# The attention output projection as seven products of quarters through one accumulator bank

## The chip, the core and the metric

The kernel runs on one core of a Trainium2 chip. The metric is the device time of one execution in microseconds; three executions of the kernel before the change took 3067.99, 3068.76 and 3071.80 us, median 3068.76 us. In addition one execution was recorded by the hardware profiler, instruction by instruction; every duration below comes from that record.

The engines are named as the profile names them: PE is the matrix engine (PEld its weight loads), DVE is VectorE, ACT is ScalarE, POOL is GpSimd, SP is SyncE, which here issues nearly all DMAs. Each engine works through its own instructions in program order; between engines, semaphores make an instruction wait for what it needs. PE writes its sums to eight PSUM banks of 128 x 512 fp32 values, and DVE and ACT read them from there.

## What is computed

Two layers. Layer 0 is a small graph attention; the change does not touch it. Layer 1 is a transformer block with a modulated layer norm, for four batches of 1024 rows of 512 values, 16 heads of 64:

```python
mod = jax.nn.silu(c) @ W_mod + b_mod
sh_msa, sc_msa, g_msa, sh_mlp, sc_mlp, g_mlp = jnp.split(mod, 6, axis=-1)
x = x + g_msa * _attention(_modulate(_layernorm(x), sh_msa, sc_msa), W_qkv, W_out, b_out)
x = x + g_mlp * _ff(_modulate(_layernorm(x), sh_mlp, sc_mlp), W1, b1, W2, b2)
```

with

```python
def _attention(x, W_qkv, W_out, b_out):
    q, k, v = jnp.split(x @ W_qkv, 3, axis=-1)          # each to 16 heads of 64
    attn = jax.nn.softmax(jnp.einsum('bqhd,bkhd->bhqk', q, k) * DH ** (-0.5), axis=-1)
    out = jnp.einsum('bhqk,bkhd->bqhd', attn, v).reshape(Bq, Tq, INNER)   # INNER = 1024
    return out @ W_out + b_out
```

The change concerns `out @ W_out`, the product of 1024 x 1024 by 1024 x 512 for each batch.

## The kernel before

**Stages.** Layer 0 and the modulation take the first 420 us or so, attention runs to about 2255 us, and the MLP to the end. All matmuls are fp32; the profile shows each as two records (and two weight loads).

**Attention is a row of 256 steps.** A step is one row tile of 128 queries (8 per batch) of one pair of heads (8 pairs `gp` per batch, 4 batches; `NS` = 256). Two pairs form a group `g` of 256 inner columns; there are 16 groups. Step `s` issues, in this order of the program: the transpose `turn` (L1118) of the first head of step s-1, evacuations left over in `later`, the two heads' `scores` (L1083, K = 64, two heads side by side in the array, into the four banks `psc`), their two row maxima `largest` on DVE (L1094), the exponentials `weights` on ACT (L1100), the reciprocal and the scaling `scaled` (first head L1107 on ACT, second head L1109 on POOL), the transpose of the second head of step s-1, and then the *fill* of the step.

**Transposed weights.** DVE transposes 32 x 32 blocks into a staging buffer `wd` (one per head and two row tiles, two buffers each, four in all); then SP issues four DMAs per head that bring the quarters to their partitions in `wT`. `attend` (L1045) multiplies `wT` of two row tiles by `v`, 16 matmuls of 256 columns into a bank `pav`, and ACT copies the result to `oT` (L1054).

**Fill.** What lies outside softmax is a list of entries (earliest step, latest step, units of PE time, place within the step, function): projections to q, k and v (each weight product by seven products of quarters, L498, in the two banks `q1` and `q2`, four entries in a fixed `chain`), `attend` (place 1), the output projection `project` (place 2), loads (place 0), sums and gates on POOL (place 4). `order_chain` places the chain by dynamic programming and `order_others` the rest, so that the squares of the units per step are smallest; `emit` writes a step's entries in the order of their places, where a chain entry has place 0.5, or 2.5 if the step before has one too.

**Output projection.** For each group, `project(b, g, n)` multiplies one row tile of the two pairs' `oT` by two 128-row pieces of `wout` (two matmuls of 512 columns, accumulated in a bank), and DVE adds the bank to the residual rows `xr[b, n]` (L1071). `wout` was multiplied by the gate g_msa on POOL beforehand (L959), and `xr` got the gated bias (L969). `pav` and `pout` share two banks under one tag, `mm`. After the last group of a batch, the rows' statistics are taken and the rows stored to `x2d`.

**MLP.** The next block of 512 rows is prepared in four pieces: `norm_T` transposes a piece in four 128-column matmuls on PE into one of two banks alternately (L408), and DVE applies scale and shift (L415). This is called in `between()`, after the first of the seven down products.

Of the kernel before, what the change touches and what calls it, by code (L numbers as in the profile page):

```python
# [41 lines left out]
def cond_block_kernel(  # L42
# [879 lines left out]
    ps = pctx.enter_context(tc.tile_pool(name="ps2", bufs=1, space=PSUM))  # L922
    with ExitStack() as actx:
        ap_ = actx.enter_context(tc.tile_pool(name="ap", bufs=1, reuse_waits="tile"))
        MM = dict(tag="mm", bufs=2)
        q1, q2 = (ps.tile([P, F], F32, name=n, tag=n) for n in ("q1", "q2"))
        two_banks = {"ma": q2, "mb": q1, "mc": q1, "md": q2}
        NP = 2 * NGRP
# [6 lines left out]
        wout, gate = {}, {}  # L935
        vt, oT, xr, wn, wd, wT = {}, {}, {}, {}, {}, {}

        def bank(name):
            return ps.tile([P, F], F32, name=name, **MM)

        turns = []

        def bank_q(name):
# [4 lines left out]

        def load_out(b, g):

            t = op_.tile([P, 2, F], F32, name="wout", tag="wout", bufs=1)
            nc.sync.dma_start(t, w_out[g * GW : (g + 1) * GW, :].rearrange("(c p) f -> p c f", p=P))
            wout[b, g] = t

# [3 lines left out]
            for p in range(2):  # L958
                nc.gpsimd.tensor_tensor(t[:, p, :], t[:, p, :], gate[b][0], ALU.mult)  # L959

        def load_rows(b, n):

            t = op_.tile([P, F], F32, name="xr", tag="xr", bufs=NT)
            nc.sync.dma_start(t, x1d[b * NT + n])
            xr[b, n] = t

        def gate_rows(b, n):

            nc.gpsimd.tensor_tensor(xr[b, n], xr[b, n], gate[b][1], ALU.add)  # L969


        def gates_of(b):
# [62 lines left out]
                rhs=lambda which, n, c: of_weights(("v", b, g), wv[b, g], which, c),  # L1035
            )

        def attend(b, gp, k):

            po = ps.tile([P, QB], F32, name="pav", **MM)  # L1040
            g, p = divmod(gp, 2)
            w = wT[b, gp, k]
            for m in range(KC):
                for j in range(2):
                    nc.tensor.matmul(  # L1045
                        po[j * D : (j + 1) * D, :],
                        lhsT=vt[b, g][:, m, p * P + j * D : p * P + (j + 1) * D],
                        rhs=w[:, j, :, m, :],
                        start=(m == 0),
                        stop=(m == KC - 1),  # L1050
                    )
            if k == 0:
                oT[b, gp] = op_.tile([P, S], F32, name="oT", tag="oT", bufs=3)
            nc.scalar.copy(  # L1054
                oT[b, gp][:, k * QB : (k + 1) * QB].rearrange("p (t u q) -> p u t q", t=QT, u=4),
                po.rearrange("p (u t q) -> p u t q", t=QT, u=4),
            )

        def project(b, g, n):

            po = ps.tile([P, F], F32, name="pout", **MM)
            for p in range(2):
                nc.tensor.matmul(  # L1063
                    po,
                    lhsT=oT[b, 2 * g + p][:, n * P : (n + 1) * P],
                    rhs=wout[b, g][:, p, :],
                    start=(p == 0),
                    stop=(p == 1),
                )
            t = xr[b, n]  # L1070
            nc.vector.tensor_tensor(t, po, t, ALU.add)  # L1071
            if g == NGRP - 1:
                i = b * NT + n
                statistics(t, mv2[:, i, :], op_)
                nc.sync.dma_start(x2d[i], t)


        def scores(b, gp, t):
# [32 lines left out]
        def turn(b, gp, t, j):  # L1111

            k, at = divmod(t, QT)
            if at == 0:
                wd[j] = ap_.tile([P, 4 * KC, QT, U], F32, name="wd", tag=f"wd{j}", bufs=2)
                if j == 0:
                    wT[b, gp, k] = ap_.tile([P, 2, 4, KC, QT * U], F32, name="wT", tag="wT", bufs=2)
            nc.vector.transpose(wd[j][:, :, at, :], wn.pop((b, gp, t, j)).rearrange("p (m k) -> p m k", k=U))  # L1118
# [9 lines left out]
            return lambda: qp.tile([P, S], F32, name="ex", tag=tag, bufs=2)  # L1128

        def home_o():  # L1130
            return op_.tile([P, S], F32, name="ex", tag="oT", bufs=3)

        def home_v():
            return vp.tile([P, NT, GW], F32, name="hs", tag="v", bufs=2)
# [10 lines left out]
        NS = B * NP * NT  # L1145
        LAG = 4

        chain = []
# [18 lines left out]
        for b in range(B):  # L1167
# [22 lines left out]
            for gp in range(NP):  # L1190
# [13 lines left out]

                for k in range(NB):
                    lo = at + QT * k + LAG
                    add(lo, lo + (lo < NS - 8), 2, 1, attend, b, gp, k)
                if p == 1:
                    for n in range(NT):
                        lo = at + max(QT * (n // 2) + LAG + 2 + (g == 0), 7)  # L1210
                        hi = at + 19
                        if at == NS - NT:

                            lo = hi = NS + (-2, -1, -1, 0, 1, 1, 3, 3)[n]
                        add(lo, hi, 1, 2, project, b, g, n)
                if gp == 0:
                    lo = max(at - 1, 0)
                    add(lo, lo, 0, 0, gates_of, b)
                    for n in range(NT):

                        lo = at + (1 + n if b == 0 else 14 + n // 2)
                        add(lo, lo, 0, 0, load_rows, b, n)
                        add(lo + 1, lo + 1, 0, 4, gate_rows, b, n)
                if p == 0:
                    add(at + 12, at + 12, 0, 0, load_out, b, g)
                    add(at + 13, at + 13, 0, 4, gate_out, b, g)
# [23 lines left out]
        add(NS - 7, NS - 7, 0, 0, put_w1_rows)  # L1250
        add(NS - 8, NS - 8, 0, 4, mlp_rows)
        for i in range(4):
            at = NS - (10, 9, 6, 4)[i]
# [17 lines left out]


        where = [f[0] for f in fill]
        inside = set(chain)

        def takes(k):

            return fill[k][2], int(k not in inside and fill[k][3] in (1, 2))

        def load_of(ks):  # L1280
            used = {}
# [3 lines left out]
            return used  # L1285

        def cost_of(u, n):
            return u * u + 4 * max(n - 2, 0) ** 2

        def order_chain():  # L1290

            used = load_of(k for k in range(len(fill)) if k not in inside)
            values = {where[k] for k, f in enumerate(fill) if f[3] == 1}
            first_steps = set(range(0, len(chain), 4))
            best = {(0, 0): (0, ())}
            for s in range(-8, NS):
                new = {}
                for (n, was), (cost, at) in best.items():
                    load, banks = used.get(s, (0, 0))
                    for m in range(2):  # L1300
                        extra = 0
                        if m > 0:
                            if n == len(chain) or not fill[chain[n]][0] <= s <= fill[chain[n]][1]:
                                break
                            load += fill[chain[n]][2]
                            if was and n not in first_steps and s not in values:
                                extra = 3
                        if n + m < len(chain) and fill[chain[n + m]][1] <= s:
                            continue
                        c = cost + cost_of(load, banks) + extra  # L1310
                        if (n + m, m) not in new or c < new[n + m, m][0]:
                            new[n + m, m] = c, (at, (s,) * m)
                best = new
            at = min((best[k] for k in best if k[0] == len(chain)), key=lambda v: v[0])[1]
            slots = []
            while at:
                at, part_ = at
                slots.append(part_)
            for k, s in zip(chain, [s for part_ in reversed(slots) for s in part_]):
                where[k] = s  # L1320
# [21 lines left out]
                    used[where[k]] = used.get(where[k], (0, 0))[0] + u, used.get(where[k], (0, 0))[1] + n  # L1342

        for _ in range(4):
            order_chain()
            order_others()
        for k, n, late in behind:
            where[k] = where[n] + late
# [12 lines left out]
        def emit(a, b):  # L1361


            for s in range(a, b):
                steps = {where[k] for k in chain}

                def place(k):
                    if k in inside:
                        return 2.5 if s - 1 in steps else 0.5
                    return fill[k][3]  # L1370

                for k in sorted(fill_of(s), key=lambda k: (place(k), k)):
                    fill[k][4]()
                if s in steps and s - 1 not in steps and sum(fill[k][2] for k in fill_of(s)) >= 3:
                    while later:
                        later.pop(0)()

        row_sum(0, 2)
        emit(-3, 0)
        before = None  # L1380
        for s in range(NS + 1):
# [4 lines left out]
            if s < NS:  # L1386
                b, r = divmod(s, NP * NT)
                gp, t = divmod(r, NT)
                sc = scores(b, gp, t)
                mx = [largest(sc[j]) for j in range(2)]  # L1390
                ws = [weights(sc[j], mx[j]) for j in range(2)]
                now = ((b, gp, t), ws)
                scaled(0, *ws[0])
# [38 lines left out]
    with ExitStack() as mctx:  # L1432
# [53 lines left out]
        for k in range(NB2):  # L1486
# [33 lines left out]
            def between():  # L1520
                if nxt < NB2:
                    for c in range(FC):
                        norm_T(1, nxt, c, new_bank, on_act=False)
                if k * VB % NT == 0:
                    spread(2, b, gate2)
                    spread(3, b, bias2)
# [79 lines left out]
```

## Time and profile before

| | |
|---|---|
| median of three executions | 3068.76 us |
| profiled execution, its time | 3070.33 us |
| profiled execution, span from first to last instruction | 3068.5 us |
| granted PE clock, mean | 0.999 of full |
| output projection on PE (L1063), records, mean of one | 512, 609 ns |
| adds of it on DVE (L1071) | 128, 678 ns |
| maxima on DVE (L1094) | 512, 1211 ns |
| transposes on DVE (L1118) | 512, 1237 ns |
| scaling on POOL (L1109) | 256, 2843 ns |
| sums of quarters on POOL (L469 to L472, 128x256) | 33 each for q and k, 728 to 730 ns |
| chain that ended last, PE's share | 82% |

The rows of a group say how long one instruction was in flight. Matmuls are pipelined, so the time that a matmul takes from PE is the distance between the starts of two that follow each other, not the 609 ns of the table. In a timeline row the columns are: start and length in us, engine, line, operation, what it writes and reads, shapes, how many were merged, and in brackets the idle time of the engine before it with what ended it.

### The profile page before, as it was taken

How to read it: one execution, taken by the hardware profiler on the slowest of the kernel's cores; microseconds unless marked ns; L12 is line 12 of the kernel's file. 1: busy time of each engine (PE TensorE's matmuls, PEld its weight loads, DVE VectorE, ACT ScalarE, POOL GpSimd, SP SyncE). 2: the span in 40 equal slices, each digit the busy share in tenths (PEclk: the TensorE clock that was granted, in tenths of full speed). 3: DMA queues.
4: the chain of work that ended last, by engine and by line, in shares of the span. 5: the costliest groups of instructions: out<-in, count | busy, mean ns of one | idle time of the engine just before them, and what ended most of it. 6: DMA issues, size and time to landing. Idle time of an engine off the chain costs nothing.

```text
span 3068.5 us, 40812 instructions
## 1 busy us (share of the span) xinstructions
PE 3032.4 (99%) x14977; PEld 1921.3 (63%) x14977; DVE 1972.2 (64%) x2759; ACT 1423.0 (46%) x2351; POOL 1212.8 (40%) x742
## 2 busy tenths in 40 slices
PE   9999999999999999999999999999999999999999
PEld 5666655455455455455455455455468888888888
DVE  3788867777878777878777878777864232223222
ACT  2444455555755555755555756556641221112211
POOL 1444456454555555555545555555531100111010
PEclk9999999999999999999999999999999999999999
DMA  6343448667777777777776777776872010101110
GB/s 194 123 131 107 137 100 202 154 159 174 190 182 189 176 168 168 194 181 181 181 174 161 197 184 175 181 177 149 194 198 80 14 46 30 49 14 42 35 41 14
DMA packets 282714, 418.00 MB, mean 136 GB/s; under 512 B 28912, under 2 KB 101036, under 8 KB 282516
## 3 DMA queue, kind: packets, MB, share of 16 engines
q1 hardware_dynamic: 282268, 415.06, 53.1%
q8 instruction: 120, 1.97, 0.3%
q14 instruction: 78, 0.64, 0.1%
q10 hardware_dynamic: 248, 0.34, 0.0%
HBM read 121.09 MB, written 25.76 MB: 48 GB/s over the span
## 4 chain that ended last, share of the span: by engine, by line
PE 82%; DVE 6%; ACT 3%; POOL 2%; issue 2%; DMA 2%; SPq 2%; POOLq 0%; ACTq 0%; DVEq 0%
PE q L498 18%; PE psc L1083 15%; PE pav L1045 14%; PE pout L1063 7%; PE mbd L498 5%; PE mbu L498 5%; PE mad L498 3%; PE mau L498 3%; PE mcd L498 2%; PE mdd L498 2%; ACT w L1100 2%; PE mcu L498 2%; PE mdu L498 2%; POOL t L727 1%; PE pa L704 1%
## 5 line engine op out<-in xcount | busy, mean ns | idle before, releaser
L1109 POOL TENSOR_SCALAR w<-w,sm 128x1024 f32<-128x1024 f32 x256 | 727.8, 2843 | 849.0 <-DVE sm L1105 849.0
L1100 ACT ACTIVATE w<-psc,mx 128x1024 f32<-128x1024 f32 x512 | 571.6, 1116 | 634.0 <-DVE mx L1094 632.7
L1118 DVE STREAM_TRANSPOSE wd<-w 128x1024 f32<-128x1024 f32 x512 | 633.4, 1237 | 131.4 <-ACT w L1107 113.5
L1094 DVE TENSOR_REDUCE mx<-psc 128x1 f32<-128x1024 f32 x512 | 599.4, 1211 | 122.0 <-PE psc L1083 119.9
L1083 PE MATMUL psc<-kT,qT 64*128 64x512 f32 x2048 | 530.8, 615 | 3.1 <-ACT kT L1009 1.4
L1045 PE MATMUL pav<-wT,v 128*64 128x256 f32 x4096 | 477.0, 382 | 2.6 <-DMA wT<-wd 2.3
L1045 PEld LDWEIGHTS pav<-wT,v 128*64 128x64 f32 x4096 | 294.5, 137 | 223.2 <-issue 68.3
L1083 PEld LDWEIGHTS psc<-kT,qT 64*128 64x128 f32 x2048 | 203.7, 186 | 254.8 <-issue 145.4
L1107 ACT ACTIVATE w<-w,sm 128x1024 f32<-128x1024 f32 x256 | 291.6, 1139 | 0.0
L477 POOL TENSOR_TENSOR tx<-hT 128x512 f32<-128x512 f32 x8 | 10.2, 1269 | 600.8 <-DVE hT L415 600.8
L1063 PE MATMUL pout<-wout,oT 128*128 128x512 f32 x512 | 245.5, 609 | 0.0
L498 PE MATMUL q<-hT,wqk 128*128 128x512 f32 (+1 forms) x396 | 182.6, 585 | 4.5 <-DVE q L512 4.5
L1063 PEld LDWEIGHTS pout<-wout,oT 128*128 128x128 f32 x512 | 90.2, 189 | 134.0 <-issue 119.0
L520 ACT COPY mbu<-mau 128x512 f32<-128x512 f32 x30 | 17.2, 572 | 276.4 <-PE mau L498 276.4
L704 PE MATMUL pa<-kp,sfT 128*128 128x320 f32 x512 | 143.5, 433 | 1.7 <-ACT sfT L679 1.7
L1071 DVE TENSOR_TENSOR xr<-pout,xr 128x512 f32<-128x512 f32 x128 | 85.5, 678 | 79.8 <-PE pout L1063 79.7
L498 PEld LDWEIGHTS q<-hT,wqk 128*128 128x128 f32 x396 | 73.5, 190 | 100.7 <-issue 86.5
L498 PE MATMUL q<-tx,ex 128*128 128x512 f32 (+1 forms) x264 | 125.0, 597 | 0.4 <-POOL tx L477 0.4
L704 PEld LDWEIGHTS pa<-kp,sfT 128*128 128x128 f32 x512 | 94.8, 190 | 38.5 <-ACT sfT L679 2.2
L664 PE MATMUL pf<-wx,xT 128*128 128x512 f32 x256 | 116.2, 597 | 0.9 <-DVE pf L653 0.9
L498 PE MATMUL mad<-w,hs 128*128 128x256 f32 x512 | 113.1, 379 | 0.0
L498 PEld LDWEIGHTS mad<-w,hs 128*128 128x128 f32 x512 | 97.3, 190 | 13.2
(285 smaller groups left out, 4234.5 us busy)
## 6 DMA issues: line engine op xcount, KB each, us to landing
wT<-wd SPq DMA_DIRECT2D x1024, 256.0 KB
wqk<-in_w_qkv SPq DMA_DIRECT2D x64, 256.0 KB
xT<-in_xt SPq DMA_DIRECT2D x32, 256.0 KB
xs<-in_x SPq DMA_DIRECT2D x32, 256.0 KB
x1d<-xs SPq DMA_DIRECT2D x32, 256.0 KB
xl<-x1d SPq DMA_DIRECT2D x32, 256.0 KB
wv<-in_w_qkv SPq DMA_DIRECT2D x32, 256.0 KB
xr<-x1d SPq DMA_DIRECT2D x32, 256.0 KB
```

The costliest lines, as they stand in the source:

```text
L498: nc.tensor.matmul(t[:, q * width : (q + 1) * width], lhsT=lhs(which, q, k), rhs=rhs(which, q, k), start=(fresh and q == 0 and k == 0), st ...
L664: nc.tensor.matmul(pfs[i], lhsT=xT[i][:, c, :], rhs=wx[:, c, :], start=False, stop=(c == FC - 1), skip_group_check=True,)
L704: nc.tensor.matmul(pas[i][:, n, :HF], lhsT=sfT2[i][:, c, :], rhs=kp[:, b, c, n * HF : (n + 1) * HF], start=False, stop=(c == FC - 1), skip ...
L1045: nc.tensor.matmul(po[j * D : (j + 1) * D, :], lhsT=vt[b, g][:, m, p * P + j * D : p * P + (j + 1) * D], rhs=w[:, j, :, m, :], start=(m == 0),
L1063: nc.tensor.matmul(po, lhsT=oT[b, 2 * g + p][:, n * P : (n + 1) * P], rhs=wout[b, g][:, p, :], start=(p == 0), stop=(p == 1),)
L1071: nc.vector.tensor_tensor(t, po, t, ALU.add)
L1083: nc.tensor.matmul(sc[j][:, n * F : (n + 1) * F], lhsT=qT[b, gp][q, t * P : (t + 1) * P], rhs=kT[b, gp][q, n * F : (n + 1) * F], start=Tru ...
L1094: nc.vector.tensor_reduce(mx, sc, axis=AX.X, op=ALU.max, negate=True)
L1100: nc.scalar.activation(w, sc, AF.Exp, bias=mx, accum_out=sm)
L1107: nc.scalar.mul(w, w, sm)
L1109: nc.gpsimd.tensor_scalar(w, w, sm, None, ALU.mult)
L1118: nc.vector.transpose(wd[j][:, :, at, :], wn.pop((b, gp, t, j)).rearrange("p (m k) -> p m k", k=U))
```

## The change

**Output projection.** For 15 of the 16 groups, `project` is replaced by `out_step`. The rows of a batch are taken in two halves `u` of 512 rows. Each half of the group's product (512 x 256 by 256 x 512) is cut into quarters and made by seven products instead of eight (Winograd's form of Strassen's scheme): `out_sums` makes three sums of quarters of `oT` (and changes one quarter in place), `out_weights` three of `wout`, both on POOL, four instructions each. Each product is two matmuls of 256 columns that fill one bank `pu`. The products are ordered so that the bank accumulates from one to the next; after each, DVE adds the whole bank to one quarter of `xr`. The last group keeps `project`.

**Banks.** The tag `mm` with its two banks goes; `pu` and `pav` get one bank each.

**Placing.** The 14 entries of a group (0.5 units each) form a second chain `outs` that `order_chain` places too, now with up to two in a step. If a step has two, `early` issues the first right behind the step's maxima. The weights in the search change as well. `attend` of the seventh pair of each batch is cut in two halves in two steps.

**Buffers.** The staging buffers `wd` of both heads share three instead of four; `wout` has two buffers and is loaded four steps earlier; `xr` holds two row tiles a tile; `oT` is six tiles of half the size.

**MLP.** In `between()`, `norm_T` applies scale and shift on ACT for all four pieces in the first block and for every second piece in the others.

```diff
-            t = op_.tile([P, 2, F], F32, name="wout", tag="wout", bufs=1)
+            t = op_.tile([P, 2, F], F32, name="wout", tag="wout", bufs=2)
...
-            t = op_.tile([P, F], F32, name="xr", tag="xr", bufs=NT)
-            nc.sync.dma_start(t, x1d[b * NT + n])
+            t = op_.tile([P, 2, F], F32, name="xr", tag="xr", bufs=NT // 2)
+            for r in range(2):
+                nc.sync.dma_start(t[:, r, :], x1d[b * NT + 2 * m + r])
...
-            po = ps.tile([P, QB], F32, name="pav", **MM)
+            if a == 0:
+                pav[0] = ps.tile([P, F], F32, name="pav", tag="pav")[:, :QB]
+            po = pav[0]
...
+        PU = ((1, 1, (0, 0)), (0, 1, (0, 0)), (5, 0, (0, 1)), (6, 0, (1, 1)), (3, 0, (1, 0)), (4, 1, (1, 1)), (2, 0, (0, 1)))
+        def out_weights(b, g):
+            w = wout[b, g]
+            wsum[b, g] = op_.tile([P, 3 * HB], F32, name="wsum", tag="wsum", bufs=1)
+            o = [wsum[b, g][:, k * HB : (k + 1) * HB] for k in range(3)]
+            sums_b(nc.gpsimd, o, w[:, 0, :HB], w[:, 0, HB:], w[:, 1, :HB], w[:, 1, HB:])
+        def out_sums(b, g, u):
+            osum[b, g] = op_.tile([P, 3 * HB], F32, name="osum", tag="osum", bufs=1)
+            o = [osum[b, g][:, k * HB : (k + 1) * HB] for k in range(3)]
+            l, r = (oT[b, 2 * g + p, u] for p in range(2))
+            sums_a(nc.gpsimd, o, l[:, :QB], r[:, :QB], l[:, QB:], r[:, QB:])
+        def out_step(b, g, u, k):
+            which, fresh, (i, j) = PU[k]
+            if fresh:
+                pu[0] = ps.tile([P, F], F32, name="pu", tag="pu")
...
+            for q in range(2):
+                nc.tensor.matmul(
+                    pu[0][:, q * HB : (q + 1) * HB],
+                    lhsT=a[:, q * P : (q + 1) * P],
+                    rhs=r,
+                    start=(bool(fresh) and q == 0),
+                    stop=True,
+                    skip_group_check=True,
+                )
+            o = xr[b, 2 * u + i][:, :, j * HB : (j + 1) * HB]
+            nc.vector.tensor_tensor(o, pu[0].rearrange("p (r f) -> p r f", r=2), o, ALU.add)
...
-                wd[j] = ap_.tile([P, 4 * KC, QT, U], F32, name="wd", tag=f"wd{j}", bufs=2)
+                wd[j] = ap_.tile([P, 4 * KC, QT, U], F32, name="wd", tag="wd", bufs=3)
...
+                    for u in range(2):
+                        for k in range(len(PU)):
+                            lo, hi = ((at + 8, at + 12), (at + 12, at + (15 if at == NS - 3 * NT else 17)))[u]
+                            if k == 0:
+                                behind.append((len(fill), len(fill) + 1, 0))
+                                add(-1, -1, 0, 4, out_sums, b, g, u)
+                            outs.append(len(fill))
+                            add(lo + k, hi + k, 0.5, 2, out_step, b, g, u, k)
...
         def cost_of(u, n):
-            return u * u + 4 * max(n - 2, 0) ** 2
+            return u * u + 4 * max(n - 1, 0) ** 2
...
-                    for m in range(2):
-                        extra = 0
+                    for m in range(2 if apart else 3):
+                        extra = 0.2 * (m == 2)
...
                 def place(k):
                     if k in inside:
-                        return 2.5 if s - 1 in steps else 0.5
+                        at = 2.5 if s - 1 in steps else 0.5
+                        return at if k in chain else min(at, 2) + 0.1 if s in steps else 2
...
+        def early(s):
+            two = [k for k in outs if where[k] == s]
+            if len(two) > 1:
+                fill[two[0]][4]()
+                done_early.add(two[0])
...
                 sc = scores(b, gp, t)
                 mx = [largest(sc[j]) for j in range(2)]
+                early(s)
                 ws = [weights(sc[j], mx[j]) for j in range(2)]
...
-                        norm_T(1, nxt, c, new_bank, on_act=False)
+                        norm_T(1, nxt, c, new_bank, on_act=(k == 0 or c % 2 == 1))
```

More of the change, by code (lines that the diff above doesn't have):

```diff
@@ L924, in cond_block_kernel @@
         ap_ = actx.enter_context(tc.tile_pool(name="ap", bufs=1, reuse_waits="tile"))
-        MM = dict(tag="mm", bufs=2)
         q1, q2 = (ps.tile([P, F], F32, name=n, tag=n) for n in ("q1", "q2"))
@@ L936, in cond_block_kernel @@
         vt, oT, xr, wn, wd, wT = {}, {}, {}, {}, {}, {}
-        def bank(name):
-            return ps.tile([P, F], F32, name=name, **MM)
         turns = []
@@ L959, in gate_out, with load_rows, gate_rows @@
                 nc.gpsimd.tensor_tensor(t[:, p, :], t[:, p, :], gate[b][0], ALU.mult)
-        def load_rows(b, n):
-            t = op_.tile([P, F], F32, name="xr", tag="xr", bufs=NT)
-            nc.sync.dma_start(t, x1d[b * NT + n])
-            xr[b, n] = t
-        def gate_rows(b, n):
-            nc.gpsimd.tensor_tensor(xr[b, n], xr[b, n], gate[b][1], ALU.add)
+        def load_rows(b, m):
+            t = op_.tile([P, 2, F], F32, name="xr", tag="xr", bufs=NT // 2)
+            for r in range(2):
+                nc.sync.dma_start(t[:, r, :], x1d[b * NT + 2 * m + r])
+            xr[b, m] = t
+        def gate_rows(b, m, r):
+            nc.gpsimd.tensor_tensor(xr[b, m][:, r, :], xr[b, m][:, r, :], gate[b][1], ALU.add)
         def gates_of(b):
@@ L1036, in v_steps, with attend @@
             )
-        def attend(b, gp, k):
-            po = ps.tile([P, QB], F32, name="pav", **MM)
+        pav = {}
+        def attend(b, gp, k, a=0, z=KC):
+            if a == 0:
+                pav[0] = ps.tile([P, F], F32, name="pav", tag="pav")[:, :QB]
+            po = pav[0]
             g, p = divmod(gp, 2)
             w = wT[b, gp, k]
-            for m in range(KC):
+            for m in range(a, z):
                 for j in range(2):
@@ L1051, in attend @@
                     )
-            if k == 0:
-                oT[b, gp] = op_.tile([P, S], F32, name="oT", tag="oT", bufs=3)
+            if z < KC:
+                return
+            u, i = divmod(k, 2)
+            if i == 0:
+                oT[b, gp, u] = op_.tile([P, F], F32, name="oT", tag="oT", bufs=6)
             nc.scalar.copy(
-                oT[b, gp][:, k * QB : (k + 1) * QB].rearrange("p (t u q) -> p u t q", t=QT, u=4),
+                oT[b, gp, u][:, i * QB : (i + 1) * QB].rearrange("p (t u q) -> p u t q", t=QT, u=4),
                 po.rearrange("p (u t q) -> p u t q", t=QT, u=4),
@@ L1059, in project @@
         def project(b, g, n):
-            po = ps.tile([P, F], F32, name="pout", **MM)
+            name = ("pu", "pav")[n % 2]
+            po = ps.tile([P, F], F32, name=name, tag=name)
             for p in range(2):
@@ L1064, in project @@
                     po,
-                    lhsT=oT[b, 2 * g + p][:, n * P : (n + 1) * P],
+                    lhsT=oT[b, 2 * g + p, n // 4][:, n % 4 * P : (n % 4 + 1) * P],
                     rhs=wout[b, g][:, p, :],
@@ L1069, in project, with rows_out @@
                 )
-            t = xr[b, n]
+            t = xr[b, n // 2][:, n % 2, :]
             nc.vector.tensor_tensor(t, po, t, ALU.add)
[L1072 to L1075, printed above, removed]
+            rows_out(b, n)
+        def rows_out(b, n):
+            t, i = xr[b, n // 2][:, n % 2, :], b * NT + n
+            statistics(t, mv2[:, i, :], op_)
+            nc.sync.dma_start(x2d[i], t)
@@ new lines, in cond_block_kernel @@
+        osum, wsum = {}, {}
+        PU = ((1, 1, (0, 0)), (0, 1, (0, 0)), (5, 0, (0, 1)), (6, 0, (1, 1)), (3, 0, (1, 0)), (4, 1, (1, 1)), (2, 0, (0, 1)))
[9 more added lines that the diff above has]
+            sums_a(nc.gpsimd, o, l[:, :QB], r[:, :QB], l[:, QB:], r[:, QB:])
@@ new lines, in cond_block_kernel @@
+        pu = {}
+        def out_step(b, g, u, k):
+            which, fresh, (i, j) = PU[k]
+            if fresh:
+                pu[0] = ps.tile([P, F], F32, name="pu", tag="pu")
+            if which in SUM_A:
+                a = osum[b, g][:, SUM_A[which] * HB : (SUM_A[which] + 1) * HB]
+            else:
+                h, f = {0: (0, 0), 1: (0, 1), 3: (1, 1), 6: (1, 0)}[which]
+                a = oT[b, 2 * g + f, u][:, h * QB : (h + 1) * QB]
+            if which in SUM_B:
+                r = wsum[b, g][:, SUM_B[which] * HB : (SUM_B[which] + 1) * HB]
+            else:
+                f, h = {0: (0, 0), 1: (1, 0), 2: (1, 1), 6: (0, 1)}[which]
+                r = wout[b, g][:, f, h * HB : (h + 1) * HB]
+            for q in range(2):
[9 more added lines that the diff above has]
+            nc.vector.tensor_tensor(o, pu[0].rearrange("p (r f) -> p r f", r=2), o, ALU.add)
@@ L1130, in home_o @@
         def home_o():
-            return op_.tile([P, S], F32, name="ex", tag="oT", bufs=3)
+            return op_.tile([P, 3 * HB], F32, name="ex", tag="wsum", bufs=1)
         def home_v():
@@ L1146, in cond_block_kernel @@
         LAG = 4
-        chain = []
+        chain, outs = [], []
         def add(lo, hi, units, place, f, *args):
@@ L1206, in cond_block_kernel @@
                     lo = at + QT * k + LAG
+                    if gp == NP - 2:
+                        for h in range(2):
+                            add(lo + h, lo + h, 1, 1, attend, b, gp, k, h * KC // 2, (h + 1) * KC // 2)
+                        continue
                     add(lo, lo + (lo < NS - 8), 2, 1, attend, b, gp, k)
-                if p == 1:
+                if p == 1 and at == NS - NT:
                     for n in range(NT):
[L1210 to L1215, printed above, removed]
+                        lo = NS + (-2, -1, -1, 0, 1, 1, 3, 3)[n]
+                        add(lo, lo, 1, 2, project, b, g, n)
+                elif p == 1:
+                    if outs:
+                        behind.append((len(fill), outs[-1], 0))
+                        add(-1, -1, 0, 4, out_weights, b, g)
+                    else:
+                        add(at + 6, at + 6, 0, 4, out_weights, b, g)
+                    for u in range(2):
[6 more added lines that the diff above has]
+                            add(lo + k, hi + k, 0.5, 2, out_step, b, g, u, k)
+                            if g == NGRP - 1 and k >= 5:
+                                for r in range(2):
+                                    behind.append((len(fill), outs[-1], 1))
+                                    add(-1, -1, 0, 4, rows_out, b, 4 * u + 2 * (6 - k) + r)
                 if gp == 0:
@@ L1218, in cond_block_kernel @@
                     add(lo, lo, 0, 0, gates_of, b)
[L1219 to L1223, printed above, removed]
+                    for m in range(NT // 2):
+                        lo = at + (1 + m if b == 0 else (12, 12, 17, 18)[m])
+                        add(lo, lo, 0, 0, load_rows, b, m)
+                        for r in range(2):
+                            add(lo + 2 + r, lo + 2 + r, 0, 4, gate_rows, b, m, r)
                 if p == 0:
-                    add(at + 12, at + 12, 0, 0, load_out, b, g)
-                    add(at + 13, at + 13, 0, 4, gate_out, b, g)
+                    add(at + 8, at + 8, 0, 0, load_out, b, g)
+                    add(at + 9, at + 9, 0, 4, gate_out, b, g)
         add(3, 3, 0, 4, rstd, rs1, mv1, nm1, NT, NTA)
@@ L1252, in cond_block_kernel @@
         for i in range(4):
-            at = NS - (10, 9, 6, 4)[i]
+            at = NS - (10, 9, 6, 3)[i]
             home = (home_ex, home_q("qT"), home_q("kT"), home_o)[i]
@@ L1273, in cond_block_kernel @@
         where = [f[0] for f in fill]
-        inside = set(chain)
+        inside = set(chain) | set(outs)
         def takes(k):
-            return fill[k][2], int(k not in inside and fill[k][3] in (1, 2))
+            return fill[k][2], int(fill[k][3] == 1)
         def load_of(ks):
@@ L1287, in cost_of, with order_chain @@
         def cost_of(u, n):
-            return u * u + 4 * max(n - 2, 0) ** 2
-        def order_chain():
-            used = load_of(k for k in range(len(fill)) if k not in inside)
+            return u * u + 4 * max(n - 1, 0) ** 2
+        def order_chain(chain, apart):
+            used = load_of(k for k in range(len(fill)) if k not in set(chain))
             values = {where[k] for k, f in enumerate(fill) if f[3] == 1}
+            others = {where[k] for k, f in enumerate(fill) if f[3] in (2, 3) and k not in set(chain)}
             first_steps = set(range(0, len(chain), 4))
@@ L1299, in order_chain @@
                     load, banks = used.get(s, (0, 0))
-                    for m in range(2):
-                        extra = 0
+                    for m in range(2 if apart else 3):
+                        extra = 0.2 * (m == 2)
                         if m > 0:
-                            if n == len(chain) or not fill[chain[n]][0] <= s <= fill[chain[n]][1]:
+                            if n + m > len(chain) or not fill[chain[n + m - 1]][0] <= s <= fill[chain[n + m - 1]][1]:
                                 break
-                            load += fill[chain[n]][2]
-                            if was and n not in first_steps and s not in values:
+                            load += fill[chain[n + m - 1]][2]
+                            if apart and was and n not in first_steps and s not in values:
                                 extra = 3
+                            if not apart and s in values and s not in others:
+                                extra += 1.2
                         if n + m < len(chain) and fill[chain[n + m]][1] <= s:
@@ L1344, in cond_block_kernel @@
         for _ in range(4):
-            order_chain()
+            order_chain(chain, True)
+            order_chain(outs, False)
             order_others()
@@ L1368, in place @@
                     if k in inside:
-                        return 2.5 if s - 1 in steps else 0.5
+                        at = 2.5 if s - 1 in steps else 0.5
+                        return at if k in chain else min(at, 2) + 0.1 if s in steps else 2
                     return fill[k][3]
                 for k in sorted(fill_of(s), key=lambda k: (place(k), k)):
-                    fill[k][4]()
+                    if k not in done_early:
+                        fill[k][4]()
                 if s in steps and s - 1 not in steps and sum(fill[k][2] for k in fill_of(s)) >= 3:
@@ L1376, in emit @@
                         later.pop(0)()
+        done_early = set()
+        def early(s):
[3 more added lines that the diff above has]
+                done_early.add(two[0])
         row_sum(0, 2)
```

## The prediction

> **What bounds the kernel now.** I read the page's busy shares first, then the busy time by stretch, the waits of the matmul engine, and one step of the attention stage instruction by instruction.
>
> ```profile
> PE 3032.4 (99%) x14977; PEld 1921.3 (63%) x14977; DVE 1972.2 (64%) x2759; ACT 1423.0 (46%) x2351; POOL 1212.8 (40%) x742
> ```
> ```profile
> 540.00:2260.00 1720.00, 1712.83 (x8772) 898.67 (x8769) 1336.10 (x1692) 1022.93 (x1591) 908.28 (x497) 1.00 0.74 177
> 2327.00:3068.50 741.50, 733.15 (x3427) 643.33 (x3425) 199.63 (x332) 140.17 (x298) 73.58 (x60) 1.00 0.10 34
> ```
> ```profile
> PE q L498 <- DVE q L512: 5.3, 6, 1.0
> PE mcu L408 <- DVE hT L415: 4.7, 7, 1.9
> ...
> PE pav L1045 <- DMA wT<-wd: 2.3, 5, 0.8
> ```
>
> PE is busy 1712.8 of 1720 us in attention (first row: length, then PE, PEld, DVE, ACT, POOL) and hardly waits for anyone: the largest waits of the whole span are 5.3 and 4.7 us. So a microsecond of matmul saved there is a microsecond of span, and a microsecond of PE waiting is a microsecond lost. VectorE is at 78% there, POOL at 53%.
>
> Now one step (a row tile's scores for two heads, and what is filled in behind them), on PE and on VectorE:
>
> ```profile
> 998.69 1.99 PE L1083 MATMUL psc<-kT,qT 64*128 64x512 f32 x8
> 1000.60 1.98 PE L1063 MATMUL pout<-wout,oT 128*128 128x512 f32 x4
> 1002.42 1.88 PE L498 MATMUL q<-tx,ex 128*128 128x512 f32 x4
> 1004.14 1.88 PE L498 MATMUL q<-hT,wqk 128*128 128x512 f32 x4
> 1005.95 1.99 PE L1083 MATMUL psc<-kT,qT 64*128 64x512 f32 x8
> ```
> ```profile
> 1000.71 2.36 DVE L1094 TENSOR_REDUCE mx<-psc 128x1 f32<-128x1024 f32 x2 [2.23 <-PE psc L1083]
> 1003.21 0.16 DVE L1105 RECIPROCAL sm<-sm 128x1 f32<-128x1 f32 x1
> 1003.41 1.25 DVE L1118 STREAM_TRANSPOSE wd<-w 128x1024 f32<-128x1024 f32 x1
> 1004.58 0.12 DVE L1105 RECIPROCAL sm<-sm 128x1 f32<-128x1 f32 x1
> 1004.62 0.67 DVE L1071 TENSOR_TENSOR xr<-pout,xr 128x512 f32<-128x512 f32 x1
> ```
>
> PE runs its chunks back to back, 7.26 us from scores to scores. VectorE sits idle 2.23 us until the scores are there, then takes both maxima, until 1003.07: 2.46 us after PE has gone on (1000.60). The projection's add comes at 1004.62, four microseconds after its matmuls began. Nobody waits for it, because the projections alternate between two banks. The trace has 26 steps of this make-up; all last 7.26 us and all have the maxima done at 2.46.
>
> **The change, part by part.** *Products removed.* 120 of 128 project() calls go (the last group keeps its 8). Consecutive full-width weight loads of 512 columns stand 0.43 us apart, so one call (4 records) is 1.71 us: 120 x 1.71 = -205.2 us.
>
> *Products added.* 15 groups x 2 halves x 7 = 210 out_step() calls of 2 matmuls of 256 columns, 4 records. The MLP's matmuls of that shape give the price:
>
> ```profile
> 2342.55 6.91 PE mad L498 x32
> ```
>
> 6.91/32 = 0.216 per record, 0.864 a call: 210 x 0.864 = +181.4 us. The arithmetic that is saved is thus 23.8 us. Weight loads (0.19) stay under 0.216.
>
> *Changes of array shape.* Scores, attend and full-width chunks differ in tile shape, and each passage from one to another costs about 0.2 us (the scores of one step are 4 pairs x 0.427 = 1.71, and take 1.92 to the next chunk). The built program has 629 such passages in the attention steps instead of 613, attend of the seventh head pair being cut in two: 16 x 0.21 = +3.4 us.
>
> *The one bank.* All seven products of a half go through one bank `pu`, and VectorE adds the bank to xr after each; a product may not write before the add of the one before has read. In the changed program's order, 155 of the 210 products have other PE work between them and their predecessor that is long enough: attend (3.6 us, half of it 1.9), two weight products (3.4) or scores. The other 55 stand directly behind their predecessor, and that stands directly behind the scores: scores, O, O, q, q. Their first matmul waits for the add of the first O; on VectorE that add stands behind the same step's two maxima, in all 55. Worked out with the step above, counted from the end of the scores: maxima done 2.46, add 0.68 (L1071's mean 678 ns) to 3.15, release of PE about 0.05 (a transpose behind L415 starts 55 ns after it), so 3.2. Without a wait the second O would have started at 0.864. Stall 2.35 us, and behind it on PE stand that O, two q chunks and the next scores: nothing else fills it. 55 x 2.35 = +129.3 us. From below: the earliest end of the maxima in any of the 256 steps is 1.98, stall 1.87, +103; nearer to nothing it can't come, as the maxima read the scores and the queue is in order. From above: maxima that start as late as the latest kind of step shows on average (0.75 instead of 0.10), 55 x 0.65 more, +165. I take 129, as the 26 steps that these 55 resemble most never start late.
>
> [...]
>
> *Adds.* 218 adds instead of 128 (each product is added): 90 x 0.678 = 61 us more on VectorE, from 1336 to 1397 of 1720 us; idle time covers that on average. Not in the 13 steps that hold O, half an attend, O: PE needs 1.92 + 2 x 0.86 + 1.87 + 2 x 0.21 = 5.9 us, VectorE 2 x 1.237 + 2 x 1.211 + 2 x 0.144 + 2 x 0.678 = 6.5: 13 x 0.6 = +8 us (bounds 0 and +20, if the wait doubles).
>
> *Sums on POOL.* 12 per group of 128x256 at 0.73 us, 15 groups: 131 us more on 908 of 1720. They queue behind the step's scaling (2.84), which starts some 4.9 us after the scores (4.2 in the step above, and the new add before it), so the second sum ends at 4.9 + 2.84 + 1.46 = 9.2. The first product that reads it is the third of a half. In 26 of the 30 halves that comes two or more steps after the sums are issued, and nothing waits; in four (the second half of the third group of each batch) it opens the very next step, some 6.5 us on: 4 x 2.8 = +11 us (bounds 0 and +27, if POOL's bursts of eight sums, in 16 steps, also cost 1 us each).
>
> *Three staging buffers.* The first head's transposed weights must have been copied out when the second head's of the next pair is first written. By the trace's events the copies land 7.0 to 8.7 us after the transposes, and the second head's write came 0.5 us or more after that, in half of all pairs over 2.2. So nothing; longer steps add room. If copies landed 2 us later, some 45 of 126 transposes would wait up to 1.5 us on VectorE; with half of that reaching PE, +20.
>
> *SyncE and loads.* The same bytes. wout loads come four steps earlier into a second buffer, xr two tiles at a time; stores of x2 wait for their statistics on SyncE as before. Nothing; at worst one attend late per batch, +4.
>
> *MLP.* Per row block, PE's third and fourth set of transposes waits for VectorE to empty a bank:
>
> ```profile
> 2426.77 0.42 PEld L408 LDWEIGHTS mcu<-ident,xl 128*128 128x128 f32 x4 [0.71 <-DVE hT L415]
> 2427.49 0.42 PEld L408 LDWEIGHTS mau<-ident,xl 128*128 128x128 f32 x4 [0.30 <-DVE hT L415]
> ```
>
> With odd pieces on ScalarE the second wait goes (0.3 x 6), the first stays, since piece 0 is still VectorE's; in the first block all four go to ScalarE and the wait of 1.9 may shrink to 0.5. -3.2 us (bounds -7 and +2).
>
> *Waits that go.* Each kind of step against its shortest, the 256 steps hold 37 us of small waits, mostly where steps under 5.7 us make scores wait for softmax to free its banks. Such steps fall from 77 to 49 in the new order: -37 x 28/77 = -13 (bounds -37 and 0).
>
> Sum: -205.2 + 181.4 + 3.4 + 129.3 + 8 + 11 - 3.2 - 13 = +111.7. The profiled execution's span is 3068.5, its time 3070.3 (1.8 around it), the median of the runs 3068.76: **3180 us**.
>
> **Rivals.** (a) *The stalls are partly free.* All the 37 us of small waits vanish, as a stall lets softmax catch up, and VectorE's short steps cost nothing: 3180 - 24 - 8 = 3148. For: PE's wait is time for VectorE and ScalarE. Against: the 55 steps are long ones already, and the small waits sit in other places. (b) *VectorE or POOL becomes the bound in more steps.* The upper bounds of adds, POOL and staging together, 12 + 16 + 20: 3228; with late maxima (36), 3264. For: 81% busy, eight sums of 5.8 us behind one scaling. Against: the steps grow longer, which gives both more time. (c) *Faster:* VectorE gets to the first O's add before PE would want the bank back. Place: the 55 pairs; price 2.35 each; it decides when a stall is under 0.32 us, the sum of all else, 17.6, over 55; with none at all 3051. For: the edit issues the first O early, right behind the scores, and everything else together is a gain. Against: VectorE takes its instructions in order, and the two maxima alone are 2.36. (d) *No change:* a stall of exactly that size.
>
> **How the numbers follow.** Forecast 0.53; (a) 0.21; (b) 0.17; (c) 0.07; (d) 0.02. The range goes from behind (a), 3130, to the near part of (b), 3222. Within 0.2% (6 us, about what this measurement can tell from no change) only (d). Faster 0.07, same 0.02, slower 0.91.
>
> **What would show it.** In the profile after: a wait of PE, `pu` for VectorE's add, some 55 times at 2.2 to 2.5 us, about 130 in all; PE at 95% instead of 99%; steps scores-O-O-q-q of 9.6 us; records of `pu` 0.216 apart; four waits for POOL's sums of some 3 us; transposes waiting for staging copies no more than 20 us. Wrong, if that wait is under 1 us a time or the 55 add up to less than 90, or if VectorE waits for DMA or POOL by tens of microseconds more.

## The result, and the profile after

The changed kernel took 3224.78 us (median of four executions, 3219.2 to 3232.3) against 3070.16 us for the kernel before in the same runs: 1.051 times as long, 95% interval 1.049 to 1.052, or 155 us more. The forecast was 3180 us with a range up to 3222. The sign and the place of the loss were right; some 45 us were missing from the sum, and the experiments show what they are.

The busy shares on the page, and who PE waited for (line, releaser: us in total, times, longest):

```profile
PE 3062.4 (95%) x15337; PEld 1992.1 (62%) x15337; DVE 2002.9 (62%) x2833; ACT 1439.0 (45%) x2367; POOL 1339.6 (42%) x922
```
```profile
PE pu L1121 <- DVE xr L1130: 59.4, 31, 2.0
PE pu L1121 <- DVE sm L1160: 55.8, 30, 2.1
PE pu L1121 <- POOL osum L470: 10.6, 4, 2.6
...
PE mcu L408 <- DVE hT L415: 2.8, 6, 0.5
```

PE's share fell from 99% to 95%, and two rows that did not exist before hold 115 us: the products wait for VectorE 61 times. The 55 steps of the prediction hold 111 of them, each a wait of 1.98 to 2.07 us; the other six are short. L1160 is the reciprocal that starts as the add ends (at 691.99 and 692.07 in the step below), so both rows tell of the add L1130. The third row is POOL's sums, four times.

One step with two products, on PE and on VectorE (columns as before the change: start, length, engine, line; the bracket is the engine's idle time before):

```profile
687.10 1.99 PE L1138 MATMUL psc<-kT,qT 64*128 64x512 f32 x8
689.01 1.13 PE L1121 MATMUL pu<-wout,oT 128*128 128x256 f32 x4
692.12 1.26 PE L1121 MATMUL pu<-wsum,oT 128*128 128x256 f32 x4 [1.98 <-DVE xr L1130]
693.18 3.49 PE L498 MATMUL q<-hT,wqk 128*128 128x512 f32 x4
696.50 1.88 PE L498 MATMUL q<-hT,ex 128*128 128x512 f32 x4
698.31 1.99 PE L1138 MATMUL psc<-kT,qT 64*128 64x512 f32 x8
```
```profile
689.12 2.35 DVE L1149 TENSOR_REDUCE mx<-psc 128x1 f32<-128x1024 f32 x2 [0.58 <-PE psc L1138]
691.39 0.68 DVE L1130 TENSOR_TENSOR xr<-pu,xr 128x512 f32<-128x512 f32 x1
```

The scores end at 689.01, the first product runs at once, VectorE takes both maxima, then the add until 692.07, and the second product starts at 692.12: 3.11 us after the scores, where the prediction said 3.2. But the step lasts 11.21 us, not 9.6: the first weight product, four records, takes 3.49 us instead of 1.88. The same stretch by windows shows why (length; busy time of PE, PEld, DVE, ACT, POOL; then the granted clock of PE; share and rate of DMA):

```profile
686.17:689.58 3.41, 3.41 (x14) 1.37 (x13) 1.16 (x2) 0.60 (x1) 0.58 (x1) 1.00 0.88 212
689.58:692.99 3.41, 1.43 (x7) 0.95 (x6) 3.41 (x5) 2.62 (x5) 0.00 (x0) 1.00 0.19 56
692.99:696.40 3.41, 3.41 (x6) 1.46 (x5) 2.17 (x4) 0.82 (x1) 2.85 (x1) 0.50 0.00 0
696.40:699.82 3.42, 3.42 (x13) 1.26 (x11) 1.05 (x1) 0.60 (x1) 1.27 (x2) 1.00 0.90 150
```

In the second window PE was busy 1.43 of 3.41 us. In the third it ran at half clock, and in the fourth at full clock again. The trace's clock record has 26 such windows between 573 and 2328 us, each 3.413 us long, all on one grid of 3.413 us. With the clock at 0.50 in them, half of each is lost: 26 x 1.71 = 44 us. Of the 26, 24 follow a window with a wait of `pu` for VectorE and two a window with a wait for POOL's sums. This profiled run is the fastest of the four (3219.2 us).

### The profile page after: what moved, and what is told of

The parts are those of the page before. It is cut to its first block, busy times and chain, and to the rows that moved or that the text cites. A ratio compares the mean times of both kernels' runs of the same rounds, so it can differ in the third digit from the quotient of the medians.

```text
span 3217.4 us, 41806 instructions
## 1 busy us (share of the span) xinstructions
PE 3062.4 (95%) x15337; PEld 1992.1 (62%) x15337; DVE 2002.9 (62%) x2833; ACT 1439.0 (45%) x2367; POOL 1339.6 (42%) x922
## 4 chain that ended last, share of the span: by engine, by line
PE 79%; DVE 9%; issue 4%; ACT 3%; POOL 2%; DMA 1%; SPq 1%; DVEq 0%; POOLq 0%; ACTq 0%
PE q L498 19%; PE psc L1138 14%; PE pav L1046 13%; PE mbd L498 5%; PE mbu L498 5%; PE pu L1121 4%; DVE mx L1149 4%; PE mad L498 3%; PE mau L498 3%; PE mcd L498 2%; PE mdd L498 2%; ACT w L1155 2%; PE mdu L498 2%; PE mcu L498 2%; POOL t L727 1%
## 5 line engine op out<-in xcount | busy, mean ns | idle before, releaser
L1046 PEld LDWEIGHTS pav<-wT,v 128*64 128x64 f32 x4096 | 287.5, 137 | 228.7 <-issue 80.6
L498 PE MATMUL q<-hT,wqk 128*128 128x512 f32 (+1 forms) x396 | 198.8, 629 | 1.0 <-DVE q L512 1.0
L1130 DVE TENSOR_TENSOR xr<-pu,xr 128x512 f32<-128x512 f32 x210 | 143.5, 683 | 38.4 <-PE pu L1121 37.5
L498 PEld LDWEIGHTS q<-hT,wqk 128*128 128x128 f32 x396 | 81.1, 206 | 90.3 <-issue 86.9
L1121 PE MATMUL pu<-wsum,osum 128*128 128x256 f32 x240 | 71.1, 421 | 61.4 <-DVE sm L1160 29.0
L1121 PE MATMUL pu<-wout,oT 128*128 128x256 f32 x360 | 101.2, 404 | 23.7 <-DVE xr L1130 11.9
L1121 PEld LDWEIGHTS pu<-wout,oT 128*128 128x128 f32 x360 | 63.0, 192 | 80.4 <-issue 46.9
```

Source lines behind the costliest of these rows:

```text
L498: nc.tensor.matmul(t[:, q * width : (q + 1) * width], lhsT=lhs(which, q, k), rhs=rhs(which, q, k), start=(fresh and q == 0 and k == 0), st ...
L1046: nc.tensor.matmul(po[j * D : (j + 1) * D, :], lhsT=vt[b, g][:, m, p * P + j * D : p * P + (j + 1) * D], rhs=w[:, j, :, m, :], start=(m == 0),
L1121: nc.tensor.matmul(pu[0][:, q * HB : (q + 1) * HB], lhsT=a[:, q * P : (q + 1) * P], rhs=r, start=(bool(fresh) and q == 0), stop=True, skip ...
L1130: nc.vector.tensor_tensor(o, pu[0].rearrange("p (r f) -> p r f", r=2), o, ALU.add)
```

## The experiments

**The second product behind the weight products.** Same work, another place:

```diff
-                        return at if k in chain else min(at, 2) + 0.1 if s in steps else 2
+                        return at if k in chain else at + 0.1 if s in steps else 2
```

> In a step with two products, the second goes behind the weight products instead of ahead of them (place 2.6 instead of 2.1); the work is the same. Theory (the one bank behind the maxima, and half-clock windows of PE that the stalls set off): the 55 waits go (about 115 us of PE idle time and 11 for loads that start cold), and with them the 27 windows of 3.413 us at half clock (46 us): 3045 to 3060, granted clock 0.997 or more. Rival (the excess over the forecast is VectorE or POOL being overloaded by the adds and sums, not the clock): the waits go, the excess stays: about 3095 to 3105. Rival (the weight products must then wait for the evacuations of the step before): 3120 and more, with waits of q for L512 or ACT.

3058.70 us, 0.997 of the kernel before (0.9955 to 0.998). The 55 waits are gone, and the clock is back:

```profile
PE pu L1121 <- POOL osum L470: 10.6, 4, 2.6
...
PE pu L1121 <- DVE sm L1160: 2.8, 6, 1.0
PE pu L1121 <- DVE xr L1130: 2.0, 2, 1.0
```
```profile
core 0: 3056.2 us, clock 0.998
```

So an overload of VectorE or POOL is not the excess: with all adds and sums in place the kernel is 166 us faster than the changed one, the stalls and the clock behind them together. Three half-clock windows are left in attention, one behind each of three of the four waits for POOL.

**The add ahead of the maxima.** `early(s)` moves one line up, so VectorE adds the first product before it takes the maxima:

```diff
-                mx = [largest(sc[j]) for j in range(2)]
                 early(s)
+                mx = [largest(sc[j]) for j in range(2)]
```

> The first product's add goes ahead of the two maxima on VectorE; PE's order is the same. Theory: the second product can start when the first is done and added, about 1.9 us after the scores instead of 3.2; a wait of 0.8 to 1.0 us on PE, 55 times. If half-clock windows need an idle time of 1.8 us or more within one window of 3.413 us, none is left: 3050 + 55 = 3105, clock 0.997 or more. If the clock is lost in proportion to idle time: 3125 to 3135, clock about 0.99. If the later maxima stretch the steps: over 3140.

3138.76 us, 1.023 (1.021 to 1.024): between the forecasts.

```profile
PE pu L1121 <- DVE xr L1130: 44.6, 54, 0.9
```

The waits are as expected, 54 of 0.83 us on the mean, and the shortest scores-O-O-q-q step (O a product through `pu`, q a weight product) takes 8.32 us against 7.28 without a wait. The clock is 0.997: 45 us of idle PE in pieces of at most 0.9 us bring no half-clock window (those left in attention stand behind the four waits for POOL).

The time is 34 us above the 3105 that the theory gave. About 9 of them were in its base: it took 3050 for the kernel without stalls, and the first experiment measured 3058.70. Beside the profiled run of the first experiment, the attention steps here are 82 us longer in all: 57 in the 55 steps, 14 in the 13 steps O, half an attend, O (8.41 us on the mean against 7.32), and 11 spread over others. `early` also acts in 28 steps where the two products had other work between them, those 13 among them; there the add now puts the maxima off, and the scores wait longer for their banks (for ACT 18 times, 4.2 us in all, against once in the changed kernel). That the later maxima cause all of this is argued; no run tries it by itself.

**The first product ahead of the scores**, in the 55 steps alone, so that its add falls into VectorE's wait for the scores:

```diff
...
+                early(s, True)
                 sc = scores(b, gp, t)
                 mx = [largest(sc[j]) for j in range(2)]
                 early(s)
```

(`early(s, True)` acts only where a weight product precedes and no attend stands between.)

> In the 55 steps the first product is issued ahead of the scores, so that its add lies in the time in which VectorE waits for the scores; the second stays where it was. Theory: no waits at the 55 places, no half-clock windows: 3040 to 3055, and by the sum of the other terms under the kernel before (3070). Rival (VectorE or POOL is the bound in more steps): 3090 to 3105.

3059.53 us, 0.997 (0.996 to 0.998), clock 0.998. No waits at the 55 places; what is left of the products' waits for VectorE:

```profile
PE pu L1121 <- DVE xr L1130: 2.0, 2, 1.0
```

It is 5 to 20 us above the expectation. The likely reason is in the sum below: the waits for POOL's sums (10.6 us in this run too) and small waits that did not shrink.

**The stall kept, but filled.** Ahead of each of the 55 waiting products, PE gets eight matmuls of 128 x 128 that nobody reads:

```diff
...
+            if late:
+                t = ps.tile([P, F], F32, name="dum", tag="pav")
+                for q in range(8):
+                    nc.tensor.matmul(t[:, q % 4 * P : (q % 4 + 1) * P], lhsT=ident, rhs=ident, start=True, stop=True)
...
```

(`late` is set where the second product follows the first with nothing between them.)

> The stall stays, but in each of the 55 places eight matmuls of 128x128 that nobody reads are issued between the two products, into the other bank, about 2 us of work; the output is the same. Theory (half clock comes from idle PE): steps stay about as long as the shortest of their kind now (9.5 us), the half-clock windows go: 3175 to 3185, 40 to 46 us faster than the changed kernel though it does more work, clock 0.997 or more. Rival (the clock falls for another reason, or costs nothing): 3225 or slower.

3178.32 us, 1.036 (1.034 to 1.037): 46 us faster than the changed kernel, with 440 matmuls more. The same step as above:

```profile
686.34 1.13 PE L1125 MATMUL pu<-wout,oT 128*128 128x256 f32 x4
687.31 1.95 PE L1111 MATMUL dum<-ident 128*128 128x128 f32 x16
689.45 1.13 PE L1125 MATMUL pu<-wsum,oT 128*128 128x256 f32 x4 [0.19 <-DVE xr L1134]
690.42 1.88 PE L498 MATMUL q<-hT,wqk 128*128 128x512 f32 x4
```
```profile
core 0: 3176.5 us, clock 0.999
```

The second product starts 3.11 us after the first, as in the changed kernel; only the weight product behind it is back at 1.88 us. This separates the two prices: the stall itself, and the clock.

**A quarter filled**: the same with `range(2)`.

> As the filled stall, but with two dummy matmuls instead of eight: they fill about a quarter of each stall, so PE stays idle some 1.4 us in each of the 55 places instead of 2.0. Theory (a whole window of 3.413 us with over about 1.8 us of idle PE brings half clock for the next window; shorter stalls bring none): the same time as with eight, 3175 to 3185, clock 0.998 or more, though three quarters of the idle time stay. Rival (clock is lost in proportion to the idle time): about 3210, clock near 0.989.

3179.53 us, 1.036 (1.034 to 1.037): as fast as with eight, while PE idles about three quarters as long in each stall.

```profile
PE pu L1125 <- DVE xr L1134: 46.5, 31, 1.5
PE pu L1125 <- DVE sm L1164: 44.3, 30, 1.6
```
```profile
core 0: 3179.5 us, clock 0.998
```

91 us of idle time at VectorE's adds in pieces of about 1.5 us cost no clock (the half-clock windows left in attention are three, behind waits for POOL). So the loss is not in proportion to idle time: half clock followed 24 of the changed kernel's 55 stalls of 1.98 to 2.07 us, and no stall at VectorE's adds here, where the longest is 1.6 us.

**The MLP edit alone**, on the kernel before:

```diff
-                        norm_T(1, nxt, c, new_bank, on_act=False)
+                        norm_T(1, nxt, c, new_bank, on_act=(k == 0 or c % 2 == 1))
```

> The kernel before with the MLP edit alone (scale and shift on ScalarE in the first block and for every second piece). Theory: PE's second wait per block goes and the first block's long wait shrinks: 3 us, and as that wait of 1.9 us is followed by the one half-clock window of the kernel before outside its end, 1.5 us more: 3063 to 3067, no half-clock window at 2326 us. Rival (ScalarE is late, or the waits were hidden): 3069 to 3071.

3066.62 us, 0.999 (0.9981 to 1.0): within the expectation, but at the edge of what can be measured, as the interval reaches 1. The transposes' waits for VectorE fall from 4.7 to 2.8 us, and the half-clock window at 2326 us is gone:

```profile
2326.00:2330.00 4.00, 3.93 (x21) 3.39 (x22) 1.02 (x1) 2.12 (x3) 3.06 (x3) 1.00 0.48 139
```

**Three staging buffers alone**, on the kernel before:

```diff
-                wd[j] = ap_.tile([P, 4 * KC, QT, U], F32, name="wd", tag=f"wd{j}", bufs=2)
+                wd[j] = ap_.tile([P, 4 * KC, QT, U], F32, name="wd", tag="wd", bufs=3)
```

> The kernel before with three shared staging buffers instead of two per head, and nothing else. Theory: the copies land before the buffer is wanted: 3068 to 3071, no wait of transposes for the copies beyond the 9 us of before. Rival (three are too few): VectorE waits for the copies by some 20 to 100 us in total, and the time is 3075 or more.

3067.62 us, 0.9997 (0.9987 to 1.0006). What the transposes waited for of the copies in this run:

```profile
  DMA wT<-wd: 7.9, 9
```

7.9 us of waits for the copies against 9.2 in the kernel before. No cost of the shared buffers can be seen.

**The sums a step earlier.** On top of the first experiment, the second half's sums are issued with the last product of the first half:

```diff
-                                behind.append((len(fill), len(fill) + 1, 0))
+                                behind.append((len(fill), outs[-1] if u else len(fill) + 1, 0))
```

> The version with the second product behind the weight products, and in addition the second half's sums on POOL issued with the last product of the first half, a step earlier where they were late. Theory: the four waits of PE for POOL's sums (10.6 us) go: 3045 to 3051, faster than both kernels. Rival (POOL then delays its scaling, or the waits move elsewhere): 3056 to 3062.

3050.19 us, 0.994 (0.992 to 0.995): faster than both kernels. The row of waits for POOL's sums is gone, and no half-clock window is left in attention:

```profile
core 0: 3049.2 us, clock 0.999
```

## Why the prediction was wrong

The step that failed is the price of the stall: 55 x 2.35 counted the time in which PE stands still, and took the clock behind it as full. No term of the sum held the granted clock. Behind 24 of the 55 stalls PE ran a whole window of 3.413 us at half clock: 41 us in the profiled run, 46 between the medians of the changed kernel and of the filled stall.

| term | forecast, us | measured, us | from |
|---|---|---|---|
| 55 stalls | +129.3 | +123 | shortest step scores-O-O-q-q 9.52, with the second product behind 7.28 |
| half clock behind them | none | +46 | changed kernel less the filled stall, 3224.8 - 3178.3 (41 between the two profiled runs) |
| products, shapes, adds, small waits | -25 | -18 | attention, first to last scores, 1834.2 before, 1816.4 with the sums a step earlier |
| POOL's sums | +11 | +10.6 | the row of PE's waits |
| MLP and the end | -3.2 | -4.6 | from the last scores on, 815.9 before, 811.3 after |

The measured terms sum to 157, beside 155 between the medians.

*The one bank* was right point by point: 55 places, the add behind the two maxima, the second product 3.11 us after the scores (3.2), PE idle 2.0 us as the profile counts it (2.2 to 2.5 were announced; the row starts only at the modelled end of the first product, 690.14 in the step shown, and not at the 0.864 us of the sum). The filled stall, in which that mechanism stands without the half clock, came out at 3178 where the forecast was 3180. That it is so close is partly luck: the stalls are 6 us under their forecast, and the products with the small waits gained 7 less than theirs.

*The clock.* The trace of before held what was needed. PE's longest wait for VectorE there was 1.9 us, in the MLP's first block; I read that row and priced its removal at 1.4 us. The windows of that stretch, of the kernel before:

```profile
2323.02:2326.43 3.41, 1.47 (x13) 0.99 (x11) 3.38 (x5) 0.53 (x1) 0.00 (x0) 1.00 0.00 0
2326.43:2329.84 3.41, 3.41 (x10) 2.92 (x11) 1.58 (x2) 0.00 (x0) 2.58 (x3) 0.50 0.47 164
```

One wait of 1.9 us, then one window at half clock. 55 new waits of nearly the same length should have been priced with it. How many of them would be followed by half clock, one case could not tell: all 55 would have added 94 us, the 24 counted afterwards add 41 and give 3221.

*Products, shapes, adds, small waits.* The small waits did not fall by 13. In the version with neither stalls nor late sums each kind of step against its shortest still holds 38 us (35 to 37 before): there are fewer short steps, but those with two products bring waits of their own (11 us in the 51 steps O, q, q, O). The saved arithmetic itself is there: with each step taken at the shortest of its kind, the attention steps are 21 us shorter in sum than before, where products and shapes were forecast at -205.2 + 181.4 + 3.4 = -20.4.

*POOL's sums* came as forecast. *MLP* did in size, in part by luck: with the MLP edit alone the stretch from the last scores on is 3.9 us shorter (815.9 to 812.0), and 1.7 of them are the half-clock window that went, for which the sum had no term. *Staging* showed no cost, as forecast. *SyncE and loads* were not tried by themselves; no row of waits names them.

Of the rivals, (a) is refuted: the 55 stalls cost about what they were forecast at. (b) named a time nearer to the result, 3228, but its causes are not there: with the products in other places, the same adds, sums and buffers run at 3059 us. (c) is what becomes of the edit once the stalls are taken out: 17.6 us of gain were forecast for all else with POOL's waits in, 10 measured.

## What to carry to other kernels

Here a bank used again at once made PE wait for its reader (55 waits of 1.98 to 2.07 us), and the reader's price was all that its engine had queued ahead of it, two maxima of 2.35 us in the step shown; put other work of PE between the two uses (3058.70 us here), or give the reader a place ahead of that queue (3138.76 here). In this kernel the waits of 1.98 to 2.07 us had to be priced with the clock behind them, half for a window behind 24 of the 55, and not only with their length; those of about 1.5 us (a quarter filled, clock 0.998) cost their length alone. Whether several shorter waits in one window add up, no run tried. Before forecasting new stalls, look for an old one of the same length and read the granted clock of the window after it.

## What the runs showed of the hardware

In the traces of the two kernels the clock went to half for whole windows of 3.413 us (the one in which a run ends is left out here). In the changed kernel there are 27 of them, between 89 and 2328 us: the first and the last start 656 windows apart, 3.4133 us each, and all the others stand on this grid to 0.004 us. By the trace's idle times of PE in the window before, of the changed kernel's windows at full clock all 22 with 1.98 us or more of idle time were followed by half clock, five of the nine with 1.82 to 1.95 us, and none with less; in the kernel before, one with 1.94 us was, the one at 2323 us. Each time a single window followed, with at most 0.25 us of idle time in it. In the run with the add ahead of the maxima, a half-clock window with 0.68 us of idle time in it, in a wait for POOL, was followed by a second one:

```profile
830.14:833.55 3.41, 2.73 (x8) 1.71 (x10) 0.62 (x2) 0.00 (x0) 1.99 (x3) 0.50 0.94 198
833.55:836.97 3.42, 3.42 (x15) 1.69 (x12) 3.22 (x5) 2.12 (x3) 0.00 (x0) 0.50 0.34 95
```

Of the changed kernel's 55 stalls, the 21 with 1.98 us or more inside one window of the grid were followed by half clock, three of the seven with 1.82 to 1.95 us, and none of the 27 with less. So equal steps took 9.58 us and 11.21 us close to each other. The clock can also explain why the changed kernel's executions spread over 13 us where the kernel before spread over 4: their granted clocks go from 0.985 to 0.982, by my estimate worth about 10 us (0.003 of 3217).
